# Graph attention with a sparse winner: index arithmetic on GpSimd, x loaded later, adj in halves and quarters, and another order of the drain

## The chip, the cores and the metric

The kernel runs on one core of one Trainium2 chip. The metric is the time of one execution on the device in microseconds (us). A profiled execution also gives a span, from the first to the last instruction of the core; the time on the device is a little longer than the span. Engines are named as in the profile: PE is TensorE (matmul), PEld its weight load, DVE VectorE, ACT ScalarE, POOL GpSimd, and SP SyncE, which here only issues transfers.

## The reference

One layer of graph attention with a residual and a layer norm:

```
ht  = (x @ W) per head                   # x 4096x512, W 512x(4*512)
e   = leaky_relu(src_i + dst_j) + adj    # adj 4096x4096
att = softmax(e, axis=-1)
y   = mean over heads of (att @ ht)
out = layernorm(x + y)
```

The entries of `adj` are either 0 or random numbers of up to 1e9. The largest entry of a row therefore outweighs all others by far more than the attention logits can reach, so the softmax of row i is 1 at the column of that entry and 0 elsewhere. Then `y[i]` is `x[col(i)] @ mean_h(W_h)`. The kernel computes this, and proves with a bound on the logits that every row has such a winner; if one had none, a general routine would follow, which is not entered with these inputs.

## The kernel before

Rows are taken in 32 blocks of 128; the row of partition p in block b is 32p + b. A block's `adj` is a tile of 128 x 4096 numbers of 4 bytes, 2 MB. All 32 blocks of x, and later of the output, live in one large tile, `hold`; W lies at first in the half of `hold` where x of blocks 16 to 31 will come. The order of all instructions on each engine is written out by hand, and each engine runs its own in order.

The main loop runs over steps t = 0 to 31. In a step:

- SP issues, when the table `x_at` says so, a load of x for four blocks (`load_x`, L109, 1 MB), and then the load of adj for block t+5 (`load_adj`, L106) into one of six buffers. Blocks 0 and 31 are loaded in four pieces, the others in one.
- DVE takes the maximum of each of 64 segments of 64 columns (`segment_maxima`, L149, two reductions a block), then finds the largest segment (`find_segment`, L156 and L158) and the number of its row in a table of segments (`row`, L160). POOL gathers that segment for all 128 rows (`lead`, L162).
- Between the two reductions DVE finds, for block t-2, the place inside the gathered segment (`find_column`, L176 and L181) and the column number (`col`, L183); POOL gathers the row of x with that number (`y`, L170).
- For block t-3, PE turns y (`project`, L206), ACT copies it out (`yt`, L213), PE adds x with an identity matrix (residual, L199) and multiplies with the mean of W (L219, eight instructions).
- For block t-4, ACT takes sum and sum of squares (`stats`, L231 and L233). For two blocks, t-6 and t-5, every second step, the normalisation factor is made (`rstd`: Sqrt on ACT L236, reciprocal and product on DVE L237 and L238), and ACT writes the normalised rows (`finish`, L242).
- `row_norm` (L226) squares and sums rows of x on ACT for the bound; `bound` (three parts), `test` and `count` make from it the proof that each row has a winner.

After the loop comes the drain: the columns of the last two blocks, of which block 31 is searched in its whole row of 4096 (`find_column_in_row`, L191), so that it needn't wait for its segment; the last blocks' projection and normalisation (`finish_last` with bn_stats, L248 to L257); and the stores of `hold` (L260): blocks 0 to 23 singly on SP, 24 to 27 in one of 1 MB, and the last four singly, the last of them on ACT's queue.

Of the kernel before, what the change touches and what calls it, by code (L numbers as in the profile page):

```python
# [9 lines left out]
F32 = mybir.dt.float32  # L10
U32 = mybir.dt.uint32
# [6 lines left out]
EPS = 1e-5  # L18
LOWEST = -3.4028234663852886e38
P = 128  # L20
# [45 lines left out]
def leading_rows(ctx, tc, x, adj, W, a, out, ident, v, n_bad, any_bad):  # L66
# [11 lines left out]
    AHEAD = 5  # L78
    Q = 4
    PIECES = 4  # L80

    once = ctx.enter_context(tc.tile_pool(name="once", bufs=1))
    adj_pool = ctx.enter_context(tc.tile_pool(name="adj_pool", bufs=AHEAD + 1))
# [14 lines left out]

    adj_t = {}

    def load_adj(ib):
        if 0 <= ib < NB:
            t = adj_t[ib] = adj_pool.tile([P, N], F32, name="adj_t")
            n = PIECES if ib in (0, NB - 1) else 1
            for k in range(n):
                nc.sync.dma_start(t[:, ts(k, N // n)], adj_rows[ib][:, ts(k, N // n)])  # L106

# [14 lines left out]
        load_adj(ib)  # L122

    make_identity(nc, ident)
    first_i = once.tile([P, NB], I32, name="first_i")
    nc.gpsimd.iota(first_i, pattern=[[S, NB]], base=0, channel_multiplier=NB * S)
    first = once.tile([P, NB], F32, name="first")
    nc.gpsimd.tensor_copy(first, first_i)
    ones = once.tile([P, P], F32, name="ones")
    nc.gpsimd.memset(ones, 1.0)  # L130
    eps = once.tile([P, 1], F32, name="eps")
    nc.gpsimd.memset(eps, EPS)

# [4 lines left out]
    sd = once.tile([P, NB], F32, name="sd")  # L138
    lead_by = once.tile([P, 1], F32, name="lead_by")

    seg_of, at_of, lead_of, y_t, o_ps = {}, {}, {}, {}, {}

    def segment_maxima(ib, lo, hi):

        if lo == 0:
            seg_of[ib] = small.tile([P, S], F32, name="seg")
        n = PIECES if ib in (0, NB - 1) else 2
        for k in range(lo * n // PIECES, hi * n // PIECES):
            nc.vector.tensor_reduce(  # L149
                seg_of[ib][:, ts(k, S // n)],  # L150
                adj_t[ib][:, ts(k, N // n)].rearrange("p (s e) -> p s e", e=E), axis=AX.X, op=OP.max,
            )

    def find_segment(ib):
        seg = seg_of.pop(ib)
        nc.vector.max(out=top[:, ib, :], in_=seg)  # L156
        at = small.tile([P, 8], U32, name="at")
        nc.vector.max_index(at, top[:, ib, :], seg)  # L158
        row = small.tile([P, 1], U32, name="row")
        nc.vector.tensor_tensor(row, at[:, 0:1], first[:, ib : ib + 1], op=OP.add)  # L160
        lead = small.tile([P, E], F32, name="lead")
        nc.gpsimd.indirect_dma_start(  # L162
            out=lead, out_offset=None, in_=adj_segs,
            in_offset=bass.IndirectOffsetOnAxis(ap=row[:, :1], axis=0),
        )
        at_of[ib], lead_of[ib] = at, lead

    def gather_rows(ib, col):
        y = y_t[ib] = rows.tile([P, D], F32, name="y", bufs=4)
# [5 lines left out]
    def find_inner(ib):  # L175
        nc.vector.max(out=inner[:, ib, :], in_=lead_of[ib])  # L176

    def find_column(ib):
        find_inner(ib)
        within = small.tile([P, 8], U32, name="within")  # L180
        nc.vector.max_index(within, inner[:, ib, :], lead_of.pop(ib))  # L181
        col = small.tile([P, 1], U32, name="col")
        nc.vector.scalar_tensor_tensor(  # L183
            col, at_of.pop(ib)[:, 0:1], float(E), within[:, 0:1], op0=OP.mult, op1=OP.add
        )
        gather_rows(ib, col)

    def find_column_in_row(ib):

        col = small.tile([P, 8], U32, name="col")  # L190
        nc.vector.max_index(col, top[:, ib, :], adj_t[ib])  # L191
        gather_rows(ib, col)

    def project(ib, between=(), order="turn residual"):

        o = o_ps[ib] = psum.tile([P, D], F32, name="o")

        def residual():
            nc.tensor.matmul(o, ident, hold[:, ib, :], start=True, stop=False)  # L199

        if order == "residual turn":
            residual()
        y = y_t.pop(ib)
        tp = psum.tile([P, KB, P], F32, name="tp", bufs=2)
        for kb in range(KB):
            nc.tensor.transpose(tp[:, kb, :], y[:, ts(kb, P)], ident)  # L206
        yt = rows.tile([P, KB, P], F32, name="yt")
        if order == "residual turn":
            half = KB // 2
            nc.scalar.copy(yt[:, :half, :], tp[:, :half, :])  # L210
            nc.vector.tensor_copy(yt[:, half:, :], tp[:, half:, :])
        else:
            nc.scalar.copy(yt, tp)  # L213
        if order == "turn residual":
            residual()
        for some in between:
            head_vector(*some)
        for kb in range(KB):
            nc.tensor.matmul(  # L219
                o, yt[:, kb, :], w_sum[:, kb, :],  # L220
                start=(kb == 0 and order == "turn"), stop=(kb == KB - 1),
            )

    def row_norm(ib):
        sq = rows.tile([P, D], F32, name="sq")
        nc.scalar.activation(sq, hold[:, ib, :], AF.Square, accum_out=xx[:, ib : ib + 1])  # L226
# [6 lines left out]
        nc.scalar.activation(sq, o, AF.Square, bias=nm[:, i], accum_out=sd[:, i])  # L233

    def rstd(i):
        nc.scalar.activation(sd[:, i], sd[:, i], AF.Sqrt, bias=eps, scale=1.0 / D)  # L236
        nc.vector.reciprocal(sd[:, i], sd[:, i])  # L237
        nc.vector.tensor_mul(nm[:, i], nm[:, i], sd[:, i])  # L238

    def finish(ib):  # L240
        i = slice(ib, ib + 1)
        nc.scalar.activation(hold[:, ib, :], o_ps.pop(ib), AF.Identity, bias=nm[:, i], scale=sd[:, i])  # L242
# [16 lines left out]
    def store(queue, lo, n):  # L259
        queue.dma_start(out_rows[:, ds(lo, n), :], hold[:, ds(lo, n), :])  # L260
# [25 lines left out]
    def head_vector(kb, h, wt):  # L286

        for k in range(KB):
            nc.tensor.matmul(  # L289
                pv[:, kb, h : 2 * H : H], wt[:, k, :], at_d[:, k, h : 2 * H : H],  # L290
                start=(k == 0), stop=(k == KB - 1),
            )
# [45 lines left out]
    def count():  # L338
        pg = psum.tile([1, NB], F32, name="px", bufs=1)
        nc.tensor.matmul(pg, ones[:, 0:1], gap, start=True, stop=True)  # L340
        nc.vector.tensor_scalar(n_bad, pg, -1.0, float(P), op0=OP.mult, op1=OP.add)
        total = once.tile([1, 1], F32, name="total")
        nc.vector.tensor_reduce(total, pg, axis=AX.X, op=OP.add)
        nc.vector.tensor_scalar(any_bad, total, -1.0, float(N), op0=OP.mult, op1=OP.add)

    x_at = {1: 1, 4: 2, 8: 3, 11: 4, 14: 5, 18: 6, 21: 7}
    norms_at = {t: [t - 2] for t in range(2, 18)}
    for k in range(8):
        norms_at[20 + k] = [16 + 2 * k, 17 + 2 * k]
    vectors = [(kb, h) for kb in range(KB) for h in range(H)]  # L350
    vectors_at = {t: 2 if t < 3 else 1 for t in range(1, 15)}
    COLUMN, PROJECT, STATS, FINISH = 2, 3, 4, 6
# [1 line left out]
    for t in range(NB):  # L354
        if t in x_at:
            load_x(x_at[t])
        load_adj(t + AHEAD)
        middle = 1 if t == NB - 1 else 2
        segment_maxima(t, 0, middle)
        if t >= COLUMN:  # L360
            find_column(t - COLUMN)
        segment_maxima(t, middle, PIECES)
        find_segment(t)
        pair = t >= FINISH and t % 2 == 0
        if pair:
            rstd(slice(t - FINISH, t - FINISH + 2))
        if t < 2:
            mean_of_heads(t)
        elif t == 2:
            mean_of_heads(2)  # L370
            mean_of_heads(3)
        if t == 0:
            turn_a()
        turned = [(*vectors[0], turn_w(*vectors.pop(0))) for _ in range(vectors_at.get(t, 0))]
        if t == 16:
            head_norms()
        if 28 <= t <= 30:
            bound(t - 28)
        if t >= PROJECT:
            project(t - PROJECT, turned)  # L380
        else:
            for some in turned:
                head_vector(*some)
        if pair:
            finish(t - FINISH)
            finish(t - FINISH + 1)
        if t >= STATS:
            stats(t - STATS)
        for ib in norms_at.get(t, ()):
            row_norm(ib)  # L390

    find_column(NB - 2)
    find_column_in_row(NB - 1)
    rstd(slice(NB - FINISH, NB - FINISH + 2))
    for ib in range(NB - 2 * Q):
        store(nc.sync, ib, 1)
    finish(NB - FINISH)
    finish(NB - FINISH + 1)
    store(nc.sync, NB - 2 * Q, Q)
    project(NB - 3, order="turn")  # L400
    find_inner(NB - 1)
    test()
    stats(NB - 4)
    rstd(slice(NB - 4, NB - 3))
    finish(NB - 4)
    store(nc.sync, NB - 4, 1)
    finish_last(NB - 3, True)
    store(nc.sync, NB - 3, 1)
    project(NB - 2, order="turn")
    count()  # L410
    finish_last(NB - 2, True)
    store(nc.sync, NB - 2, 1)
    project(NB - 1, order="residual turn")
    finish_last(NB - 1, False)
    store(nc.scalar, NB - 1, 1)

# [233 lines left out]
```

## Time and profile before

| What | Value |
|---|---|
| median of 14 runs | 259.67 us (258.35 to 261.43) |
| the profiled execution's time | 259.07 us |
| its span | 257.3 us |
| PE busy | 203.4 us (79%) |
| DVE busy | 200.2 us (78%) |
| ACT busy | 115.2 us (45%) |
| POOL busy | 62.0 us (24%) |
| bytes moved | 97.76 MB, 380 GB/s over the span |
| adj loads, issue to landing, median | 33.4 us (2 MB), 6.4 us (0.5 MB) |
| gathers, issue to landing, median | 6.7 us (`lead`), 8.3 us (`y`) |
| segment maxima, 128 x 2048 | 2280 ns each, 60 of them |
| granted PE clock, mean | 0.958 |

Busy times are averages over the whole span and don't say what bounds a stage; the views that do are slices and stretches of time, and the chain of waits, which is followed back from the last instruction. A share of the DMA engines near 1 means that all 16 were transferring. A transfer's time from issue to landing includes the time that it stood behind others in its queue.

### The profile page before, as it was taken

The page shows a single profiled execution, that of the slowest core. Times are in us where ns is not written, and L with a number is a line of the kernel's source. Part 1 is how long each engine was busy: PE and PEld are TensorE (multiplying, and loading weights), DVE is VectorE, ACT ScalarE, POOL GpSimd, SP SyncE. Part 2 cuts the span into 40 slices and gives each one's busy share as a digit, 9 for nine tenths or more (in the row PEclk, how much of TensorE's full clock was granted, in tenths as well). Part 3 has the DMA queues.
Part 4 walks back from the last instruction along what each step waited for, and adds up shares of the span by engine and source line. Part 5 has one row for each costly group of instructions (what it writes and reads, how often), then busy time and mean ns, then how long its engine had stood idle before and what let it go on. Part 6 is the DMA issues. An engine that isn't in the chain of part 4 may idle for free.

```text
span 257.3 us, 2464 instructions
## 1 busy us (share of the span) xinstructions
PE 203.4 (79%) x679; PEld 101.9 (40%) x680; DVE 200.2 (78%) x387; ACT 115.2 (45%) x285; POOL 62.0 (24%) x75
## 2 busy tenths in 40 slices
PE   0199869999899899989498788897785889939760
PEld 0136327665455556645143333332332334413320
DVE  2546777469979997996989999799799999972341
ACT  2012005356646475737264537584656555642110
POOL 1101221122322322232122233313313332320000
PEclk9999779999999999999979999999999999976996
DMA  6999999999999999999999999999999999997111
GB/s 250 415 433 420 412 425 422 410 428 420 416 416 422 418 415 414 427 410 416 423 411 425 415 421 418 414 423 414 415 420 416 418 393 399 383 376 290 41 41 52
DMA packets 14995, 97.76 MB, mean 380 GB/s; under 512 B 2296, under 2 KB 2296, under 8 KB 9472
## 3 DMA queue, kind: packets, MB, share of 16 engines
q1 hardware_dynamic: 11232, 87.82, 82.8%
q0 software_dynamic: 3584, 9.44, 9.6%
q10 hardware_dynamic: 160, 0.28, 0.3%
q8 instruction: 7, 0.11, 0.2%
q14 instruction: 12, 0.10, 0.1%
HBM read 89.15 MB, written 8.39 MB: 379 GB/s over the span
## 4 chain that ended last, share of the span: by engine, by line
DMA 57%; DVE 31%; PE 5%; issue 2%; ACT 1%; SPq 1%; POOLq 0%
DMA adj_t<-in_adj_dram 55%; DVE seg L149 21%; PE o L219 5%; DVE col L191 2%; DMA y<-in_x_dram,col 1%; DVE within L181 1%; DVE at L158 1%; DVE top L156 1%; DVE st L251 1%; DVE col L183 1%; DVE inner L176 1%; DVE row L160 1%; ACT hold L242 1%; SPq L106 1%; DVE hold L248 1%
## 5 line engine op out<-in xcount | busy, mean ns | idle before, releaser
L149 DVE TENSOR_REDUCE seg<-adj_t 128x32 f32<-128x2048 f32 (+1 forms) x68 | 146.3, 2155 | 30.3 <-DMA adj_t<-in_adj_dram 30.2
L219 PE MATMUL o<-w_sum,yt 128*128 128x512 f32 x256 | 121.4, 618 | 7.2 <-ACT yt L213 6.1
L219 PEld LDWEIGHTS o<-w_sum,yt 128*128 128x128 f32 x256 | 47.6, 196 | 67.3 <-issue 48.4
L170 POOL DMA_INDIRECT y<-in_x_dram,col x32 | 30.3, 947 | 99.1 <-issue 77.0
L162 POOL DMA_INDIRECT lead<-in_adj_dram,row x32 | 30.4, 951 | 68.5 <-DVE row L160 44.2
L213 ACT COPY yt<-tp 128x512 f32<-128x512 f32 x31 | 18.2, 586 | 42.4 <-PE tp L206 42.3
L206 PE MATMUL tp<-ident,y 128*128 128x128 f32 x128 | 19.8, 277 | 17.3 <-DMA y<-in_x_dram,col 17.3
L265 PE MATMUL o<-hold,ident 128*128 128x512 f32 x32 | 20.9, 813 | 15.6 <-DMA hold<-in_L_gnn_W_dram 15.6
L199 PE MATMUL o<-hold,ident 128*128 128x512 f32 x60 | 31.3, 604 | 0.0
L206 PEld LDWEIGHTS tp<-ident,y 128*128 128x128 f32 x128 | 14.3, 141 | 30.2 <-issue 27.9
L242 ACT ACTIVATE hold<-o,nm,sd 128x512 f32<-128x512 f32 x29 | 21.1, 781 | 6.0 <-DVE nm L238 6.0
L283 ACT COPY wt<-tp 128x512 f32<-128x512 f32 x16 | 9.2, 586 | 25.5 <-PE tp L281 25.5
L226 ACT ACTIVATE sq<-hold 128x512 f32<-128x512 f32 x32 | 19.8, 619 | 1.7 <-DMA hold<-in_x_dram 1.7
L233 ACT ACTIVATE sq<-o,nm 128x512 f32<-128x512 f32 x29 | 19.9, 687 | 0.9
L289 PEld LDWEIGHTS pv<-at_d,wt 128*128 128x128 f32 x128 | 16.3, 191 | 6.8 <-issue 3.8
L265 PEld LDWEIGHTS o<-hold,ident 128*128 128x128 f32 x32 | 8.1, 264 | 25.6 <-issue 20.6
L266 ACT ACTIVATE w_sum<-o 128x512 f32<-128x512 f32 x4 | 2.4, 599 | 34.2 <-PE o L265 34.2
L231 ACT ACTIVATE sq<-o 128x512 f32<-128x512 f32 x29 | 17.5, 605 | 0.0
L289 PE MATMUL pv<-at_d,wt 128*128 128x2 f32 x128 | 15.3, 244 | 0.6 <-ACT wt L283 0.6
L281 PEld LDWEIGHTS tp<-ident,hold 128*128 128x128 f32 x64 | 7.9, 142 | 6.9 <-issue 6.9
L281 PE MATMUL tp<-ident,hold 128*128 128x128 f32 x64 | 9.3, 273 | 0.0
L199 PEld LDWEIGHTS o<-hold,ident 128*128 128x128 f32 x60 | 9.1, 191 | 0.1
(73 smaller groups left out, 94.5 us busy)
## 6 DMA issues: line engine op xcount, KB each, us to landing
adj_t<-in_adj_dram SPq DMA_DIRECT2D x30, 2048.0 KB, 33.4
hold<-in_x_dram SPq DMA_DIRECT2D x8, 1024.0 KB, 33.8
out_dram<-hold SPq DMA_DIRECT2D x27, 256.0 KB, 5.5
adj_t<-in_adj_dram SPq DMA_DIRECT2D x8, 512.0 KB, 6.4
hold<-in_L_gnn_W_dram SPq DMA_DIRECT2D x4, 1024.0 KB, 17.8
out_dram<-hold SPq DMA_DIRECT2D x1, 1024.0 KB, 6.4
lead<-in_adj_dram,row POOLq DMA_INDIRECT x32, 6.7
y<-in_x_dram,col POOLq DMA_INDIRECT x32, 8.3
```

Source lines behind the costliest of these rows:

```text
L149: nc.vector.tensor_reduce(seg_of[ib][:, ts(k, S // n)], adj_t[ib][:, ts(k, N // n)].rearrange("p (s e) -> p s e", e=E), axis=AX.X, op=OP.max,)
L162: nc.gpsimd.indirect_dma_start(out=lead, out_offset=None, in_=adj_segs, in_offset=bass.IndirectOffsetOnAxis(ap=row[:, :1], axis=0),)
L170: nc.gpsimd.indirect_dma_start(out=y, out_offset=None, in_=x, in_offset=bass.IndirectOffsetOnAxis(ap=col[:, :1], axis=0),)
L199: nc.tensor.matmul(o, ident, hold[:, ib, :], start=True, stop=False)
L206: nc.tensor.transpose(tp[:, kb, :], y[:, ts(kb, P)], ident)
L213: nc.scalar.copy(yt, tp)
L219: nc.tensor.matmul(o, yt[:, kb, :], w_sum[:, kb, :], start=(kb == 0 and order == "turn"), stop=(kb == KB - 1),)
L226: nc.scalar.activation(sq, hold[:, ib, :], AF.Square, accum_out=xx[:, ib : ib + 1])
L233: nc.scalar.activation(sq, o, AF.Square, bias=nm[:, i], accum_out=sd[:, i])
L242: nc.scalar.activation(hold[:, ib, :], o_ps.pop(ib), AF.Identity, bias=nm[:, i], scale=sd[:, i])
L265: nc.tensor.matmul(o, ident, hold[:, w_at + kb * H + h, :], start=(h == 0), stop=(h == H - 1))
L289: nc.tensor.matmul(pv[:, kb, h : 2 * H : H], wt[:, k, :], at_d[:, k, h : 2 * H : H], start=(k == 0), stop=(k == KB - 1),)
```

## The change

- `row` and `col` are computed on POOL as integer additions. A further POOL multiplication, `start`, makes 64 times the segment number ahead of time. The table `first` is made directly as integers.
- `rstd` is computed on POOL: a scale and addition, a power of -0.5, and a product. ACT's Sqrt and DVE's reciprocal and product leave the loop; they stay in the drain's `finish_last`.
- adj is loaded and reduced in halves, block 0 and the last four blocks in quarters. (Before, all but two blocks were loaded whole and reduced in halves.)
- x of blocks 4g to 4g+3 is loaded at step 4g-2, for g = 1 to 6. x of the last four blocks is loaded after all of adj. `row_norm` of a block follows its `stats`; the last four follow in the drain, and `bound` with them.
- `project` is split into `turn`, `residual` and `products`. Blocks 28 to 30 get their x by an addition on DVE in `finish_last`, block 28 now too; block 31 gets it on PE between its turn and its products.
- The drain has a new order. Blocks 0 to 11 are stored singly on SP, behind the last x. Blocks 12 to 27 are stored in four transfers of 1 MB on ACT's queue, issued behind the copy of the turned y of block 31. The last four are stored as before.

```diff
+    LATE = NB - Q
+    def pieces(ib):
+        return PIECES if ib == 0 or ib >= LATE else PIECES // 2
...
-            n = PIECES if ib in (0, NB - 1) else 1
+            n = pieces(ib)
...
-        n = PIECES if ib in (0, NB - 1) else 2
+        n = pieces(ib)
...
-        nc.vector.tensor_tensor(row, at[:, 0:1], first[:, ib : ib + 1], op=OP.add)
+        nc.gpsimd.tensor_tensor(row, at[:, 0:1], first[:, ib : ib + 1], op=OP.add)
...
+        start = at_of[ib] = small.tile([P, 1], U32, name="start")
+        nc.gpsimd.tensor_tensor(start, at[:, 0:1], width, op=OP.mult)
...
-        nc.vector.scalar_tensor_tensor(
-            col, at_of.pop(ib)[:, 0:1], float(E), within[:, 0:1], op0=OP.mult, op1=OP.add
-        )
+        nc.gpsimd.tensor_tensor(col, at_of.pop(ib), within[:, 0:1], op=OP.add)
...
-        nc.scalar.activation(sd[:, i], sd[:, i], AF.Sqrt, bias=eps, scale=1.0 / D)
-        nc.vector.reciprocal(sd[:, i], sd[:, i])
-        nc.vector.tensor_mul(nm[:, i], nm[:, i], sd[:, i])
+        nc.gpsimd.tensor_scalar(sd[:, i], sd[:, i], 1.0 / D, EPS, op0=OP.mult, op1=OP.add)
+        nc.gpsimd.tensor_tensor(sd[:, i], sd[:, i], power[:, : i.stop - i.start], op=OP.pow)
+        nc.gpsimd.tensor_mul(nm[:, i], nm[:, i], sd[:, i])
...
-    x_at = {1: 1, 4: 2, 8: 3, 11: 4, 14: 5, 18: 6, 21: 7}
-    norms_at = {t: [t - 2] for t in range(2, 18)}
-    for k in range(8):
-        norms_at[20 + k] = [16 + 2 * k, 17 + 2 * k]
+    x_at = {4 * g - 2: g for g in range(1, NB // Q - 1)}
```

The drain after the change, whole (before it: see the end of the function above):

```
load_x(NB // Q - 1)
for ib in range(3 * Q):
    store(nc.sync, ib, 1)
find_column(NB - 2)
rstd(slice(NB - FINISH, NB - FINISH + 2))
find_column_in_row(NB - 1)
turn(NB - 3)
products(NB - 3, 0, KB - 1)
finish(NB - FINISH)
finish(NB - FINISH + 1)
for ib in range(LATE, NB):
    row_norm(ib)
turn(NB - 2)
products(NB - 3, KB - 1, KB)
bound(0)
products(NB - 2)
finish_last(NB - 4, True)
find_inner(NB - 1)
bound(1)
finish_last(NB - 3, True)
bound(2)
test()
turn(NB - 1)
for g in range(3, LATE // Q):
    store(nc.scalar, g * Q, Q)
residual(NB - 1)
products(NB - 1, 0, KB - 1)
pg = count()
products(NB - 1, KB - 1, KB)
for ib in (NB - 4, NB - 3):
    store(nc.sync, ib, 1)
finish_last(NB - 2, True)
store(nc.sync, NB - 2, 1)
report(pg)
finish_last(NB - 1, False)
store(nc.scalar, NB - 1, 1)
```

## The prediction

> **What bounds the kernel now.** I read the page's slices first, then busy times in stretches, the chain of waits, the groups of DVE and GpSimd (POOL), and the timeline of the last 40 us.
>
> ```profile
> DVE  2546777469979997996989999799799999972341
> DMA  6999999999999999999999999999999999997111
> ...
> 187.00:219.00 32.00, 26.38 (x77) 11.70 (x77) 30.97 (x64) 18.19 (x47) 9.46 (x10) 1.00 1.01 409
> 219.00:232.00 13.00, 9.03 (x27) 4.18 (x26) 10.93 (x24) 6.92 (x18) 3.79 (x4) 0.88 1.03 377
> 232.00:258.00 26.00, 14.46 (x36) 5.99 (x34) 7.39 (x20) 2.87 (x9) 0.00 (x0) 0.83 0.26 100
> ```
>
> In the slices the DMA engines are full from slice 1 to slice 36 (36 x 6.43 = 231 us and some more), then nearly empty. The stretches (length; PE, PEld, DVE, ACT, POOL busy; PE clock; DMA share; GB/s) say the same: 409 and 377 GB/s up to 232 us, 100 after. So there are two stages: one with bytes as its limit, and a drain of some 20 us in which one chain of small steps runs.
>
> ```profile
> 223.75 0.22 DVE within L181
> 224.00 0.16 DVE col L183
> 224.16 4.41 DVE col L191 x2
> 228.56 0.07 DVE sd L237
> 228.66 0.17 DVE nm L238
> 228.83 0.03 issue
> 228.86 1.45 ACT hold L242 x2
> 230.31 0.48 ACT yt L213
> 230.79 0.04 issue
> 230.83 6.16 PE o L219 x8
> ...
> 239.50 3.70 PE o L219 x8
> ...
> 246.03 3.71 PE o L219 x8
> ...
> 251.24 0.81 DVE hold L257
> ```
>
> That is the drain: the column search of the last block (4.41), then the normalisation factor of blocks 26 and 27 queued behind that search on DVE, ACT's finish of them, and only then three blocks' products one after another, up to the last store at 252.1 us.
>
> When does adj end? Ahead of its last byte go 67.1 MB of adj, 4.2 of W, 8.4 of x and some 28 pairs of gathers (9.44 MB/32 = 0.295 MB a pair): 88.0 MB. The rates of the stretches 0:9, 9:40, 40:77, 77:122, 122:153, 153:187 (285, 424, 419, 418, 418, 416 GB/s) and 187:219 times their lengths give 90.2 MB by 219 us. The 2.2 MB too many are stores; 2.2/0.41 = 5 us back gives about 214 us. DVE ends the last segment maxima at 222.7 us: it sits one block behind, because a 2 MB tile counts only when it is whole (about 5.7 us of transfer, and 5.95 us of DVE work from 186.8 to 222.7 over six blocks).
>
> **What the Trainium skill says.** "GPSIMD Engine Reference", section "Performance versus the Vector engine": Pool pays two software hops per instruction and about 2.6 cycles an element of a two-input operation. At one or two elements a lane only the fixed part counts; the trace agrees in size (POOL CAST of 128x32: 211 ns, memset of one column: 93). "SBUF — State Buffer", section "SBUF: two separate sides": DVE and GpSimd share a port pair that one of them locks for a whole instruction, in DVE's case when it is in a two-port mode or has two SBUF inputs. The segment maxima read 2048 elements in 2280 ns, about 0.9 a ns, which is one port's rate, and POOL's gather starts stay at 943 to 950 ns beside them: I see no lock in this trace. "DMA: Bandwidth & Descriptors", section "Issuing engines are not separate DMA queues": transfers of SP, ACT and GpSimd run on the same 16 engines and interleave. The trace agrees: share 1.01 with GpSimd's queue at 9.6%. So no byte becomes cheaper by changing queue. "TensorE: Matmul & The Clock Gate", section "What's actually happening": after an idle window of about 3.4 us PE falls to half clock. Here PE idled some 4 us before 230.83, and the eight products took 6.16 us instead of 3.70.
>
> **The change, part by part.**
>
> *Row, column and factor to GpSimd.*
>
> ```profile
> L160 DVE TENSOR_TENSOR row<-at,first 128x1 uint32<-128x1 uint32 x32 | 5.1, 159 | 1.2
> L183 DVE SCALAR_TENSOR_TENSOR col<-at,within 128x1 uint32<-128x1 uint32 x31 | 4.9, 160 | 1.1
> L238 DVE TENSOR_TENSOR nm<-nm,sd 128x2 f32<-128x2 f32 x14 | 2.2, 161 | 0.5
> L237 DVE RECIPROCAL sd<-sd 128x2 f32<-128x2 f32 x14 | 2.2, 157 | 0.0
> ```
>
> DVE loses 5.1 + 4.9 + 2.2 + 2.2 = 14.4 us, 0.45 a block: 5.95 becomes about 5.5. Bytes set the pace at about 6.2 us a block where x is loaded and 5.7 where not, so this saves nothing directly; it keeps DVE from sliding. ACT loses its small Sqrt (0.29 x 14), which is not on the path. POOL gains three small operations a block (row, start, column) and three a pair for the factor, say 0.2 us each. Per pair POOL then has 4 gather starts x 0.95, 2.1 us of start delays (0.26 after row, 0.76 after col), 6 x 0.2 and 3 x 0.2: 7.7 us of 11.4 to 12.4. The factor waits on POOL for ACT's statistics, and the next gathers stand behind it; those statistics are a step old by then, so I count no wait. The power, on two elements a lane, has no row in this trace: not below 0.1 us (the smallest memset), and free up to about 4 us, where POOL would be full. I take 0.3. The step from index to gather start stays about equal: one hop DVE to POOL in either case, +0.1.
>
> *x later, the last four blocks' x behind adj.* Seven x loads instead of eight stand ahead of adj's end: 1.05 MB/0.41 = 2.6 us earlier. x of block 4g lands just ahead of adj of block 4g+2; PE wants it three steps after block 4g, so it is not late.
>
> *Halves and quarters.* SP issues about twice as many loads (0.33 us each, on a queue that mostly waits). Rows become 8 KB, late ones 4 KB. 9:40, where W and x in 8 KB rows are half of the bytes, ran at 424 GB/s; 219:232, mostly stores in 2 KB rows, at 377. So 8 KB costs between 0 and 3.3 us on 54 MB; I take 1.3. The late 4 KB rows cost 0 to 1.5; I take 0.7. Adj then ends at A = 214 - 2.6 + 2.0 = 213.4 us. The gain is what follows: DVE no longer begins a block when it is whole. After the last quarter come one 1.21 us reduction and 0.6 of search, were there nothing else.
>
> *The drain, counted from A.* Within the last block DVE stops for lead of block 29 (segment found about A-8.3, plus 0.3 start and 6.7 landing), until A-1.3; three quarters later, at A+2.8, the maxima are done and at A+3.4 the segment. Lead of block 30 was asked for at A-2.9 and lands at A+4.1; its column takes until A+4.7; then the 4.41 us search, A+9.2. The factor no longer queues behind it. The gather of y for block 31 starts at A+9.4 and lands in 5.6 to 8.3 us, I take 7: A+16.4, against a start at 229.3 before, now 222.8.
>
> PE: y of block 28 lands at about A+2.8, its work ends at A+8; block 29 from A+8 to A+12 with three of four products; y of block 30 lands at A+13; the four moved row norms (4 x 0.8 on ACT, behind the two finishes and a copy) end near A+14, so the moved bound's transpose goes then (0.27 on PE, its two reductions 0.5 on DVE, beside the products), and the products of block 30 (3.7) end near A+18.7. Blocks 28 and 29 are now added and normalised on DVE, 2.6 us each (0.69 + 0.69 + 0.18 + 0.29 + 0.16 + 0.55), beside PE. Block 31 is turned behind block 30's products, not when its y lands: turned and copied (0.6 + 0.6) at A+20.3. Then residual 1.0, products 3.7, count 0.2, and DVE's 0.70 + 0.19 + 0.30 + 0.17 + 0.81 with hops: the last store is ready at A+27.
>
> But ACT issues the stores of blocks 12 to 27 only behind that copy, at A+20.3, and the last store stands on ACT's queue behind them. Queue SP ends x (1.05 MB) and twelve stores (3.1 MB) with the gathers at about A+13.6: some 7 us of empty DMA. From A+20.3: 0.4 issue, about 1 to the first byte, then 4.2 MB and the last blocks' 1.05 less 0.5 that SP has stored by then, 4.7 MB at 0.40 = 11.8 us: A+33.5. What follows a last byte: before, the store's issue ended at 252.5 and the span at 257.3; less 1 to the first byte and 0.65 of transfer, 3.2 us. So the span is 213.4 + 36.7 = 250.1 us, 7.2 less than 257.3. The profiled execution took 259.07, 1.8 more than its span, and the median is 259.67, 0.6 above that: 252.5 us.
>
> **Rivals.**
>
> *The compute chain ends last* (15 in 100). If the stores of ACT finish by A+31 because some of them start sooner (y of 31 early, PE less behind), the last store decides: A+27 + 0.4 + 4.8 = A+32.2, span 245.6, 248.0 us. For it: only 4 us separate the two ends. Against: the order puts all four big stores behind the last turn.
>
> *Packets and cold PE eat half* (12 in 100). 8 and 4 KB rows at their upper bound add 2.8 us to A, and half clock on one block in the drain (6.16 - 3.70 = 2.5) passes to the stores: 252.5 + 5 = 257.5. For it: 377 GB/s with short rows, and the clock fell in this very stage before. Against: 424 GB/s with half the bytes in 8 KB rows.
>
> *GpSimd becomes the pace: slower* (11 in 100). One mechanism: the power, run per block pair in POOL's order ahead of the next gathers. Beyond the 4 us that fit, each further us costs about 13 us over 13 pairs: the 7.2 us gained are gone at about 4.6 us, and at 6 us the time is 252.5 + 26 = 278 us. For it: no such operation is in the trace and the skill calls GpSimd's loops software. Against: two elements, and all of POOL's fixed costs seen are under 0.3 us.
>
> *The gather or the drain does not move* (6 in 100): lead or y land so late that the search order counts for nothing, 259 to 260 us. Against: 4.41 us and the factor behind it are plain in the chain.
>
> **How the numbers follow.** Forecast 56 in 100, own range 249 to 256 (A by -1.5 to +2.5, start of the stores by -2 to +2). With the first two rivals 248.0 to 257.5 hold over 80 in 100. About 0.3% (0.8 us) is what can be told from no change. Faster: 56 + 15 + 12 and 1 of the last rival, 84; same 4; slower 12.
>
> **What would show it.** Right: the last segment maxima end near 216 instead of 222.7; in the slices the DMA digits fall for one slice near 228 to 233 and fill again; ACT's queue holds four 1 MB stores issued near 234; POOL's power under 1 us. Wrong: segment maxima that wait for something other than adj in mid-kernel; GB/s clearly under 410 between 40 and 190 us; POOL near full; DMA full without a gap, in which case the time is under 249.

## The result and the profile after

| | before | after |
|---|---|---|
| median | 259.45 us (47 runs) | 254.97 us (253.86 to 256.15, 10 runs) |
| ratio to before | | 0.983, 95% interval 0.980 to 0.985 |
| profiled execution, time and span | 259.07, 257.3 us | 255.6, 253.7 us |

The change makes the kernel 1.7% faster. The forecast was 252.5 us (2.7%), in a range of 248.0 to 257.5: right in direction and in its main mechanism, and too good by 2.5 us.

The slices of the changed kernel (40 of 6.34 us; digits are tenths of busy time, the last row GB/s):

```profile
DVE  2586657695999489958898989589958999845820
POOL 1203233244455345544444544525652464640000
...
DMA  7999999999999999999999999999999999980793
GB/s 251 431 417 416 413 416 412 410 415 418 408 410 408 417 411 410 414 408 414 413 415 408 413 410 411 408 417 412 413 407 403 404 401 409 403 309 29 305 413 114
```

Before, the DMA engines were full up to about 236 us and then nearly idle to the end. Now they are full up to about 226, nearly empty in one slice (29 GB/s), and full again nearly to the end. The gap that the prediction described, the empty stretch ahead of the last stores, is there, and what it said would follow it, too.

The same in stretches, for the changed kernel (length; PE, PEld, DVE, ACT, POOL busy; PE clock, DMA share, GB/s):

```profile
77.00:122.00 45.00, 45.00 (x187) 26.08 (x186) 36.43 (x56) 29.34 (x71) 20.18 (x44) 1.00 1.02 412
...
187.00:216.00 29.00, 23.34 (x67) 10.14 (x68) 24.47 (x44) 13.49 (x33) 14.29 (x31) 1.00 1.02 405
216.00:226.00 10.00, 7.77 (x19) 3.35 (x18) 7.87 (x11) 5.87 (x15) 5.46 (x13) 0.83 1.04 393
226.00:236.00 10.00, 9.33 (x32) 4.47 (x31) 4.27 (x12) 5.68 (x16) 0.93 (x1) 1.00 0.24 84
236.00:251.00 15.00, 4.64 (x12) 1.44 (x10) 5.98 (x22) 1.13 (x3) 0.00 (x0) 0.78 0.84 336
```

And for the kernel before, in two of these stretches:

```profile
77.00:122.00 45.00, 42.90 (x180) 24.79 (x179) 40.54 (x76) 27.32 (x68) 13.25 (x14) 1.00 1.01 418
...
226.00:236.00 10.00, 6.03 (x12) 2.73 (x12) 4.46 (x12) 4.37 (x9) 0.95 (x1) 0.66 1.00 380
```

Two things are to be read here. In mid-kernel the full DMA engines move 412 GB/s instead of 418, though their share is as high: the shorter rows cost something all the way. And between 226 and 236 us the load is now the other way round: PE busy 9.33 of 10 us, DMA 0.24.

The order of the drain, from the timeline of ACT of the changed kernel (ACTq is ACT's instruction queue; such a line issues a transfer):

```profile
235.95 0.59 ACT L206 COPY yt<-tp 128x512 f32<-128x512 f32 x1
235.96 3.12 ACTq L258 DMA_DIRECT2D out_dram<-hold  x4
239.42 0.29 ACT L253 ACTIVATE r<-mv,eps 128x1 f32<-128x1 f32 x1 [2.88 <-DVE mv L251]
241.71 0.29 ACT L253 ACTIVATE r<-mv,eps 128x1 f32<-128x1 f32 x1 [2.00 <-DVE mv L251]
243.08 0.34 ACTq L258 DMA_DIRECT2D out_dram<-hold  x1
```

The four 1 MB stores are issued with the copy of block 31, at 236 us. The last block's store is ready at 243.1, 9 us earlier than before (252.1), but it stands behind 4.2 MB on its own queue, and the span ends 10.6 us later. Before, 5.2 us passed from that issue to the end:

```profile
252.08 0.39 ACTq L260 DMA_DIRECT2D out_dram<-hold  x1
```

### The profile page after: what moved, and what is told of

It is laid out like the page before. It is cut to its first block, busy times and chain, and to the rows that moved or that the text cites. A ratio compares the mean times of both kernels' runs of the same rounds, so it can differ in the third digit from the quotient of the medians.

```text
span 253.7 us, 2541 instructions
## 1 busy us (share of the span) xinstructions
PE 203.4 (80%) x677; PEld 102.3 (40%) x678; DVE 189.2 (75%) x304; ACT 109.6 (43%) x266; POOL 97.9 (39%) x213
## 4 chain that ended last, share of the span: by engine, by line
DMA 43%; POOL 16%; issue 16%; DVE 9%; PE 6%; ACT 5%; POOLq 0%; DVEq 0%
DMA adj_t<-in_adj_dram 38%; DMA hold<-in_L_gnn_W_dram 6%; PE o L217 5%; POOL lead L168 5%; POOL y L178 5%; DVE seg L155 4%; POOL sd L235 2%; ACT hold L240 2%; ACT sq L224 1%; DVE st L249 1%; POOL start L173 1%; POOL row L166 1%; DVE hold L255 1%; POOL col L191 1%; DVE hold L246 1%
## 5 line engine op out<-in xcount | busy, mean ns | idle before, releaser
L217 PE MATMUL o<-w_sum,yt 128*128 128x512 f32 x256 | 123.2, 624 | 7.4 <-ACT yt L206 7.4
L178 POOL DMA_INDIRECT y<-in_x_dram,col x32 | 32.3, 1008 | 17.1 <-POOL col L191 15.2
L263 PE MATMUL o<-hold,ident 128*128 128x512 f32 x32 | 18.7, 737 | 16.0 <-DMA hold<-in_L_gnn_W_dram 16.0
L210 PE MATMUL o<-hold,ident 128*128 128x512 f32 x58 | 30.9, 615 | 0.5 <-DMA hold<-in_x_dram 0.5
L240 ACT ACTIVATE hold<-o,nm,sd 128x512 f32<-128x512 f32 x28 | 20.3, 779 | 19.9 <-POOL nm L236 19.9
L166 POOL TENSOR_TENSOR row<-at,first 128x1 uint32<-128x1 uint32 x32 | 5.9, 186 | 53.0 <-DVE at L164 51.9
L191 POOL TENSOR_TENSOR col<-start,within 128x1 uint32<-128x1 uint32 x31 | 5.9, 190 | 38.2 <-DVE within L189 37.3
L287 PEld LDWEIGHTS pv<-at_d,wt 128*128 128x128 f32 x128 | 17.2, 200 | 7.3 <-ACT wt L281 3.7
L263 PEld LDWEIGHTS o<-hold,ident 128*128 128x128 f32 x32 | 7.3, 241 | 24.7 <-POOL row L166 10.6
L229 ACT ACTIVATE sq<-o 128x512 f32<-128x512 f32 x28 | 16.9, 605 | 0.0
L287 PE MATMUL pv<-at_d,wt 128*128 128x2 f32 x128 | 16.0, 249 | 0.6 <-ACT wt L281 0.6
```

Source lines behind the costliest of these rows:

```text
L178: nc.gpsimd.indirect_dma_start(out=y, out_offset=None, in_=x, in_offset=bass.IndirectOffsetOnAxis(ap=col[:, :1], axis=0),)
L210: nc.tensor.matmul(o_ps[ib], ident, hold[:, ib, :], start=True, stop=False)
L217: nc.tensor.matmul(o_ps[ib], yt_of[ib][:, kb, :], w_sum[:, kb, :], start=(start and kb == 0), stop=(kb == KB - 1),)
L263: nc.tensor.matmul(o, ident, hold[:, w_at + kb * H + h, :], start=(h == 0), stop=(h == H - 1))
L287: nc.tensor.matmul(pv[:, kb, h : 2 * H : H], wt[:, k, :], at_d[:, k, h : 2 * H : H], start=(k == 0), stop=(k == KB - 1),)
```

## The experiments

All ratios are to the kernel before, timed beside it on the same chip, with 95% intervals. The chips differ from group to group, so kernels are compared by their ratios. Each expectation names a theory, A, and a rival.

| kernel | median us | ratio |
|---|---|---|
| after | 254.97 | 0.983 (0.980 to 0.985) |
| e1_whole: adj mostly whole | 254.42 | 0.982 (0.978 to 0.986) |
| e4_no_pool | 254.87 | 0.984 (0.980 to 0.988) |
| e7_x_early | 256.76 | 0.990 (0.986 to 0.993) |
| e9_drain_only | 255.28 | 0.983 (0.979 to 0.988) |
| e5_before_halves | 259.19 | 0.997 (0.994 to 1.000) |
| e2_stores_sp | 264.94 | 1.022 (1.018 to 1.026) |
| e6_fill: stores on SP | 249.73 | 0.961 (0.957 to 0.966) |
| e8_fill_whole | 249.08 | 0.959 (0.954 to 0.964) |
| e10_drain_filled | 254.70 | 0.979 (0.972 to 0.985) |
| e12_fill_whole_no_pool | 251.76 | 0.969 (0.964 to 0.974) |
| e11_earlier | 250.20 | 0.965 (0.960 to 0.971) |
| e13_one_factor | 251.66 | 0.974 (0.970 to 0.978) |

### Which part brings the gain

**e1_whole**, adj of blocks 1 to 27 loaded whole:

```diff
-            n = pieces(ib)
+            n = PIECES if ib == 0 or ib >= LATE else 1
             for k in range(n):
                 nc.sync.dma_start(t[:, ts(k, N // n)], adj_rows[ib][:, ts(k, N // n)])
```

> The changed kernel, but adj of blocks 1 to 27 is loaded whole again (reductions stay in halves, the last four blocks stay in quarters). Theory A (the shorter rows cost the DMA rate): 417 to 419 GB/s between 9 and 187 us instead of 411 to 416, adj's last byte some 2.5 to 3 us earlier, near 213; the drain moves less, as DVE is again most of a block behind when the late blocks come, so 252 to 255.5 us. Rival (the rate fell for another reason, such as GpSimd's instructions): the rate stays at 411 to 412 and the time rises to 256 or more, because DVE starts each block later.

The rate came back, as this stretch shows:

```profile
77.00:122.00 45.00, 43.11 (x174) 24.47 (x173) 37.35 (x57) 28.43 (x69) 21.25 (x45) 1.00 1.01 418
```

In the records of single packets adj's last one ends at 215.62 us before, at 215.59 after and at 212.98 here. So x behind adj is worth its 2.6 us, and halves alone took 2.6 us back. The time hardly moved (254.42, intervals overlap). DVE ended its maxima only 0.9 us earlier than in the changed kernel, and ACT copied block 28's turned y 0.9 us earlier. The four stores were issued 2.5 us earlier (233.45), but 1.6 of that is PE's clock: block 28's products took 3.70 us in this profile and 5.30, partly at half clock, in that of the changed kernel. A profile holds one execution, and the mean granted clock varies between executions (0.928 to 0.969 in the six of this kernel). The 0.9 us are too little for the times to tell.

**e5_before_halves**, the pieces put into the kernel before:

```diff
+    def pieces(ib):
+        return PIECES if ib == 0 or ib >= NB - Q else PIECES // 2
...
-            n = PIECES if ib in (0, NB - 1) else 1
+            n = pieces(ib)
```

(and the same in the reductions)

> The kernel before, with adj in halves and the last four blocks in quarters, nothing else. Theory A (rows cost 3 us of adj's end, but DVE no longer lags by a block): rate 411 to 412, adj ends near 218, the last maxima end near 221 instead of 222.7, time 257 to 260. Rival (the pieces carry the gain of the whole change): 256 or less.

259.19 us, a ratio of 0.997: at most 0.6% faster, of the 1.7% of the whole change. Pieces alone carry little of the gain. What the expectation says of the rate and of the maxima is left open.

**e4_no_pool**, row, column and factor back where they were:

```diff
-        nc.gpsimd.tensor_tensor(row, at[:, 0:1], first[:, ib : ib + 1], op=OP.add)
+        nc.vector.tensor_tensor(row, at[:, 0:1], first[:, ib : ib + 1], op=OP.add)
...
-        nc.gpsimd.tensor_scalar(sd[:, i], sd[:, i], 1.0 / D, EPS, op0=OP.mult, op1=OP.add)
-        nc.gpsimd.tensor_tensor(sd[:, i], sd[:, i], power[:, : i.stop - i.start], op=OP.pow)
-        nc.gpsimd.tensor_mul(nm[:, i], nm[:, i], sd[:, i])
+        nc.scalar.activation(sd[:, i], sd[:, i], AF.Sqrt, bias=eps, scale=1.0 / D)
+        nc.vector.reciprocal(sd[:, i], sd[:, i])
+        nc.vector.tensor_mul(nm[:, i], nm[:, i], sd[:, i])
```

> The changed kernel with row, column and factor back on DVE and ACT. Theory A (they only keep DVE from sliding): DVE goes from 5.45 to about 5.9 us a block, above the pace of blocks without x, so the last segment maxima end 1 to 3 us later than 218.3 and the time is 255.5 to 258. Rival (the hop through GpSimd costs as much as DVE saves: from the search to the gather's start it took about 0.8 us against 0.3 before): no difference or up to 1.5 us faster, 253.5 to 255.

254.87, as the changed kernel. Yet the search of block 31 starts 2.8 us later:

```profile
221.89 0.16 DVE L187 SCALAR_TENSOR_TENSOR col<-at,within 128x1 uint32<-128x1 uint32 x1
223.17 0.17 DVE L233 RECIPROCAL sd<-sd 128x2 f32<-128x2 f32 x1 [1.12 <-ACT sq L222]
223.37 0.16 DVE L234 TENSOR_TENSOR nm<-nm,sd 128x2 f32<-128x2 f32 x1
223.44 0.09 DVE L195 MATCH_VALUE_LOAD col<-top,adj_t 128x8 f32 x1
223.52 4.42 DVE L195 FIND_INDEX8 col<-top,adj_t 128x8 uint32<-128x4096 f32 x1
```

The factor stands ahead of the search on DVE and waits 1.1 us for ACT. So theory A's delay was there and its price was not: in this drain the search is not on the way to the end. Block 28's products, from which the end follows (see e9_drain_only), began only 0.3 us later than in the changed kernel (220.99 instead of 220.65).

**e7_x_early**, `x_at` of the kernel before, all eight loads ahead of adj's end:

```diff
-    x_at = {4 * g - 2: g for g in range(1, NB // Q - 1)}
+    x_at = {1: 1, 4: 2, 8: 3, 11: 4, 14: 5, 18: 6, 21: 7}
...
-    load_x(NB // Q - 1)
```

> The changed kernel with the loads of x at the steps of the kernel before, all eight ahead of adj's end. Theory A (bytes decide when the drain begins): adj ends 2.6 us later, near 218, and so does everything behind it: 256.5 to 258. Rival (DVE and PE are behind by more than that, so adj's last byte is not what the drain waits for): within 1 us of 255.0.

Adj's last packet 2.6 us later (218.2), as expected; the time 256.76, 0.7 points above the changed kernel's ratio, about 1.8 us of the 2.6: within theory A's range.

**e9_drain_only** undoes all three: no GpSimd arithmetic, x at the old steps, adj in the old pieces.

> The changed kernel with row, column and factor on DVE and ACT, x loaded at the old steps and adj in the old pieces: of the change only the new drain is left. Theory A (the drain is the gain, and the other parts matter little because the stores of ACT end last): 255 to 257. Rival (the parts each bring some 1 to 2 us): 257.5 to 259.5, near the kernel before.

255.28, ratio 0.983, the ratio of the whole change. The new drain alone (with the row norms in their new places, which this run keeps) brings the whole gain, and the other parts together nothing that shows. In it the search starts at 224.6 us, 3.9 us after that of the changed kernel, and the gather of y for block 31 at 229.8, and still ACT issues the four stores at the same time, from its timeline:

```profile
235.77 3.11 ACTq L256 DMA_DIRECT2D out_dram<-hold  x4
```

Block 31 is turned behind the products of block 30. The last packet of its gather ends at 232.8 us, and the turn starts at 235.1: the search and this gather have slack. PE's work from block 28 on has none. In the profiles of the changed kernel, e1, e4, e7 and e9 the stores are issued 10.0 to 10.2 us behind the end of block 28's products, and the span ends 17.5 to 18.0 us behind that. So with the stores where they are, the end moves with block 28's products.

What the new order takes out is a wait of PE. Before, it waited 3.97 us for the copy of block 29's y, which stood on ACT behind the finish of blocks 26 and 27, and so behind the 4.42 us search; here it waits 0.67. The first line is of the kernel before, the second of e9_drain_only:

```profile
230.83 6.14 PE L219 MATMUL o<-w_sum,yt 128*128 128x512 f32 x8 [3.97 <-ACT yt L213]
226.87 2.84 PE L215 MATMUL o<-w_sum,yt 128*128 128x512 f32 x6 [0.67 <-ACT yt L204]
```

What each move of the drain is worth by itself was not tried.

### The stores that the end waits for

**e2_stores_sp** moved the four large stores to SP behind the twelve single ones, a line too early.

```diff
     for ib in range(3 * Q):
         store(nc.sync, ib, 1)
+    for g in range(3, LATE // Q):
+        store(nc.sync, g * Q, Q)
...
-    for g in range(3, LATE // Q):
-        store(nc.scalar, g * Q, Q)
```

> The changed kernel, but the four 1 MB stores of blocks 12 to 27 go on SP right behind the twelve single ones instead of on ACT behind the copy of block 31. Theory A (the empty DMA from 227 to 237 us is what the end waits for): the gap fills, the last bytes are those of block 31, the last store stays ready near 243 us, span 247.5 to 249.5, time 249 to 251. Rival (the gap is needed, since the last two gathers of y are slowed by stores): y of blocks 30 and 31 lands 2 us or more later, PE waits for it, and the time is 253 or more.

264.94 us, slower than both. The kernel stores blocks 26 and 27 before they are normalised, so it leaves out the normalisation of these two in the output; and their finish, later in the program, must wait until the store has read them. Its timeline of ACT:

```profile
226.30 0.59 ACT L206 COPY yt<-tp 128x512 f32<-128x512 f32 x1 [3.91 <-PE o L217]
239.77 1.45 ACT L240 ACTIVATE hold<-o,nm,sd 128x512 f32<-128x512 f32 x2 [12.88 <-DMA out_dram<-hold]
241.11 0.62 ACT L224 ACTIVATE sq<-hold 128x512 f32<-128x512 f32 x1
```

ACT waits 12.88 us for a store, and the drain behind it. It neither supports nor refutes the gap; it shows what a store costs whose rows are still to be written.

**e6_fill** puts it right: blocks 12 to 23 behind the single stores, 24 to 27 behind the finish of block 27.

```diff
+    for g in range(3, LATE // Q - 1):
+        store(nc.sync, g * Q, Q)
...
     finish(NB - FINISH + 1)
+    store(nc.sync, LATE - Q, Q)
...
-    for g in range(3, LATE // Q):
-        store(nc.scalar, g * Q, Q)
```

> The changed kernel, with the 1 MB stores of blocks 12 to 23 on SP right behind the twelve single ones, and that of 24 to 27 on SP behind the finish of block 27; ACT issues only the last store. Theory A (the end waits for stores that were issued at 236 us into empty DMA engines): no empty stretch from 227 to 237 us, the last store still ready near 243 us and the last to land, span 247.5 to 249.5, time 249 to 251. Rival (the gap protects the last two gathers): they land 2 us or more later, PE waits for them, time 253 or more.

249.73 us, 3.9% faster than before and 2.1 points below the change. Its stretches:

```profile
216.00:226.00 10.00, 6.61 (x20) 2.65 (x18) 7.73 (x10) 6.34 (x17) 5.17 (x12) 1.00 1.04 400
226.00:236.00 10.00, 8.86 (x28) 4.26 (x29) 5.12 (x16) 5.15 (x15) 1.07 (x1) 1.00 1.02 418
236.00:251.00 15.00, 4.76 (x13) 1.51 (x11) 5.33 (x18) 1.17 (x3) 0.00 (x0) 0.77 0.30 116
```

No gap, and the last store is issued at 243.12, as in the changed kernel (243.08). 5.2 us later the span ends, not 10.6. The rival is half right. The last gather of y lands 5.3 us later than in the changed kernel (its last packet ends at 234.7 instead of 229.4), and PE waits for y of blocks 29 and 31, as it did not there:

```profile
224.85 0.63 PE L204 MATMUL tp<-ident,y 128*128 128x128 f32 x4 [0.65 <-DMA y<-in_x_dram,col]
235.41 0.63 PE L204 MATMUL tp<-ident,y 128*128 128x128 f32 x4 [0.99 <-DMA y<-in_x_dram,col]
```

That the last store is ready at the same moment all the same is due to PE's clock: block 28's products took 3.70 us in this profile, not 5.30.

**e8_fill_whole**: both e6 and e1.

> Both edits: stores filled in on SP as in e6_fill, and adj of blocks 1 to 27 loaded whole as in e1_whole. Theory A: adj ends near 213, DVE's last maxima near 217.4, the chain of PE begins about 1 us earlier, and with no stores to wait for this shows: 0.5 to 1.5 us under e6_fill, 248 to 250.5. Rival (PE's chain from block 28 on is set by something else): equal to e6_fill within 0.4 us.

249.08, the fastest median of the study. The gain of 0.65 us over e6_fill lies in theory A's range, but the intervals overlap, so it isn't shown by the times. (In this profile block 28's products took 5.40 us, again partly at half clock.)

### What the other parts are worth once the stores are out of the way

**e10_drain_filled** is e9_drain_only with the stores of e6_fill.

> e9_drain_only (row, column and factor on DVE and ACT, x at the old steps, adj in the old pieces) with the stores filled in on SP as in e6_fill. Theory A (the other parts of the change were hidden by the late stores and show once these are gone): the gather of y for block 31 starts near 229.8 us as in e9, lands some 7 us later because stores now run beside it, and the chain behind it takes 8.3 us to the last store: 245.5, time 251.5 to 253. Rival (the parts bring nothing at all): 249 to 250.3, as e6_fill and e8_fill_whole.

Ratio 0.979, against 0.959 for e8_fill_whole: with the late stores gone the other parts of the change are worth about 2 points, some 5 us. The other way round, filling in the stores without these parts gains nothing that shows (0.979 against 0.983 for e9_drain_only, intervals overlap). The time, 254.70, lies above theory A's 251.5 to 253, and in the profile that is PE's clock, as e10's timeline of PE shows:

```profile
228.44 0.67 PE L202 MATMUL tp<-ident,y 128*128 128x128 f32 x4 [2.18 <-DMA y<-in_x_dram,col]
229.78 5.49 PE L215 MATMUL o<-w_sum,yt 128*128 128x512 f32 x6 [0.68 <-ACT yt L204]
```

Six products take 5.49 us instead of 2.84 (e6_fill), after a wait of 2.18 for a late gather, a turn and a copy.

**e12_fill_whole_no_pool** is e8_fill_whole without GpSimd's arithmetic.

> e8_fill_whole with row, column and factor back on DVE and ACT. Theory A (without the late stores the work on DVE counts): the search of block 31 starts 2 to 3 us later, as it did in e4_no_pool (223.5 us against 220.7), the gather behind it too, and the time is 250 to 251.5. Rival (PE's chain covers it): 248.5 to 249.5, as e8_fill_whole.

Ratio 0.969 against 0.959, with intervals that just touch: GpSimd's part seems to be worth about a point now, where it was worth nothing under the late stores (e4). e11_earlier below, which has this part and was timed on the same chip as e12, stands at 0.965, so the point is not firm. The last maxima end at 221.6 us instead of 217.4, so DVE has slid, and the factor makes it wait once more:

```profile
222.88 0.16 DVE L187 SCALAR_TENSOR_TENSOR col<-at,within 128x1 uint32<-128x1 uint32 x1
225.81 0.17 DVE L233 RECIPROCAL sd<-sd 128x2 f32<-128x2 f32 x1 [2.76 <-ACT sd L232]
226.01 0.16 DVE L234 TENSOR_TENSOR nm<-nm,sd 128x2 f32<-128x2 f32 x1
226.08 0.08 DVE L195 MATCH_VALUE_LOAD col<-top,adj_t 128x8 f32 x1
226.16 4.42 DVE L195 FIND_INDEX8 col<-top,adj_t 128x8 uint32<-128x4096 f32 x1
```

**e13_one_factor** is e12 with this one factor on GpSimd.

> e12_fill_whole_no_pool, with the factor of blocks 26 and 27 in the drain alone on GpSimd; all other rows, columns and factors stay on DVE and ACT. Theory A (what GpSimd brings is mostly this one factor: on DVE it stood ahead of the 4.42 us search and waited 2.76 us for ACT in e12): the search of block 31 starts near 223.2 us instead of 226.2, and the ratio to the kernel before falls from 0.969 to 0.960 to 0.966. Rival (it is DVE's time in every step): the search starts at 225 us or later, ratio 0.968 to 0.972.

The search does start 4.4 us earlier (221.7), 1.3 of it because the maxima ahead of it ended earlier in this profile (220.3 instead of 221.6). But the ratio is 0.974, no lower than e12's. Theory A fell: that wait was long in one profile, and removing it doesn't show in the times. The rival's late search did not come either. The maxima still end 2.8 us later than in e8_fill_whole (217.4), which leaves DVE's time in every step as the likelier source of GpSimd's point; the runs don't settle it.

**e11_earlier** is e8 with the factor ahead of `find_segment`, block 28's column a quarter earlier, and the four row norms ahead of the turn of block 29.

> e8_fill_whole with three moves: the factor of two blocks in front of find_segment on POOL instead of behind it, the column of block 28 after the first quarter of block 30, and the four last row norms ahead of the turn of block 29 on ACT. Theory A (PE's chain from block 28 on starts with the landing of y for blocks 28 and 29): both gathers start about 1 us earlier, and the end comes 0.7 to 1.5 us earlier: 247.3 to 248.5. Rival (the last gather, behind the 4.4 us search, sets the end): within 0.4 us of e8_fill_whole.

0.965 against 0.959, intervals overlapping: no gain. The first two turns did come earlier (block 28 at 216.95 us instead of 218.51), and PE then waited for the next gathers, in its timeline:

```profile
223.18 2.84 PE L217 MATMUL o<-w_sum,yt 128*128 128x512 f32 x6 [0.80 <-ACT yt L206]
228.59 0.63 PE L204 MATMUL tp<-ident,y 128*128 128x128 f32 x4 [2.56 <-DMA y<-in_x_dram,col]
...
234.20 0.63 PE L204 MATMUL tp<-ident,y 128*128 128x128 f32 x4 [0.27 <-DMA y<-in_x_dram,col]
```

That there is no gain is as the rival said; its reason is seen only in part. In this profile PE waits for the landing of y for blocks 30 and 31, and most for block 30 (2.56 us), whose gather does not stand behind the long search. e8_fill_whole waited for neither in its profile.

## Why the prediction was right, and where it was short

- *The end is the four stores on ACT, issued at the copy of block 31, with a gap in front.* Right, and the reason why the gain is no larger: e6_fill removes it and gains 5 us more. e6_fill changes both the time and the queue of these stores, and a late issue on SP was not run; but from 237 to 248 us the changed kernel moves about 410 GB/s, the rate of full engines, so the late start is cause enough.
- *The start of these stores* was put 20.3 us behind adj's end; measured 235.96 - 215.59 = 20.4. That this fits so well is in part luck. Block 28's work ended 10.4 us behind adj's end, not 8, and from there 10.0 us passed to the issue, not 12.3, because PE did not wait for y of block 30 and the row norms as the sum had it. Two things made block 28 late. Its products took 5.30 us instead of 3.70, although PE had waited only 0.74 and 1.49 us just before, not some 4 us as in the case that the prediction cites; so 1.6 of the 2.5 us of the rival "cold PE" (half clock) happened. And the factor: the prediction let GpSimd wait for ACT's statistics and counted nothing, but the wait was the other way round. ACT's finish of blocks 24 and 25 waited 2.63 us for the factor, and the copy of block 28's y stood behind it:

```profile
216.68 1.45 ACT L240 ACTIVATE hold<-o,nm,sd 128x512 f32<-128x512 f32 x2 [2.63 <-POOL nm L236]
...
220.65 5.30 PE L217 MATMUL o<-w_sum,yt 128*128 128x512 f32 x8 [1.49 <-ACT yt L206]
```

- *The rest of the drain, counted from adj's end.* Last maxima +2.8, measured +2.7 (218.3, where "near 216" was named as a sign: adj's end was later than put). Search +4.8, measured +5.1; last store ready +27, measured +27.5. The gather of block 31 started later than the sum (+10.3 for +9.4) and landed, counted to its last packet, in 3.5 us, not 7, into engines that were almost empty by then; it had slack either way.
- *Where it was short: adj's end.* It was put at A = 213.4 from 214 before; both kernels' last packet ends at 215.6. Of these 2.2 us, 1.6 are the starting point. It was counted from bytes as if no store came before adj's last packet, but 0.76 MB of stores, 1.8 us at 0.41 MB a us, had moved by then. The rest is the term "8 KB costs between 0 and 3.3 us; I take 1.3", which measured 2.6 (e1_whole), so that the pieces gave back all that the later x had gained. It leant on the stretch 9:40 with 424 GB/s, where 8 KB rows were said to be half of the bytes; by the packet records they were a third (4.2 of 13.1 MB), and with nearly all rows at 8 KB the changed kernel moves 416 there. The late 4 KB rows, taken as 0.7, seem to cost nothing: e1_whole has them, and its adj ends 2.6 us ahead of the kernel before, all of which the later x explains (e7_x_early). They were not tried alone.
- *Where it was short: the tail of the stores.* From the stores' issue to the end of the span 17.7 us passed instead of 16.4. SP had stored one of the last blocks by the time of the issue, not two, so 5.0 MB were left instead of 4.7, and the last packets came in thinly: 13.9 us passed from the first to the last, where 11.8 were put. Adj's end, this start and this tail, 2.2 + 0.1 + 1.3 = 3.6 us, are the whole difference in the span (253.7 against 250.1). The profiled execution lay 0.6 us above its median, where that of before lay below, hence 2.5 us in the medians.
- *Two readings of the kernel before* were off without harm. The DMA engines were full to about 236 us, not 232, and the first of the 64 gather starts took 1.12 us, not 0.95.
- *Row, column and factor "save nothing directly".* Right for this kernel (e4_no_pool), and the reason was too narrow: what they save is time ahead of the search of block 31, which has slack here, while the factor on GpSimd makes ACT wait as shown above. What the power costs, taken as 0.3 us with a bound of 4, is 0.72:

```profile
L235 POOL TENSOR_TENSOR sd<-sd,power 128x2 f32<-128x2 f32 x14 | 10.1, 724 | 1.2
L173 POOL TENSOR_TENSOR start<-at,width 128x1 uint32<-128x1 uint32 x32 | 6.5, 203 | 0.6
L166 POOL TENSOR_TENSOR row<-at,first 128x1 uint32<-128x1 uint32 x32 | 5.9, 186 | 53.0 <-DVE at L164 51.9 <-DVE v L293 1.2
L191 POOL TENSOR_TENSOR col<-start,within 128x1 uint32<-128x1 uint32 x31 | 5.9, 190 | 38.2 <-DVE within L189 37.3 <-PE tp L279 0.8
```

These groups of POOL (busy us and mean ns of one behind the bar) put the slower rival away: POOL is busy 39% of the span, and the small operations are 0.19 to 0.20 us, as assumed. The step from a search to its gather did stay about equal, as put (+0.1): in the medians it grew from 0.46 to 0.78 us for `lead` and fell from 0.96 to 0.81 for `y`.
- *The compute chain ends last* (15 in 100, 248.0 us): not in this kernel, but it is what e6_fill and e8_fill_whole become, at 249.7 and 249.1.

## What to carry to other kernels

When a drain has both stores and a chain of small steps, issue every store whose rows are final as soon as the queue's last load is issued. Here four stores queued behind an unrelated late step cost about 5 us at the end. But stores that fill the gap slow the last gathers: without the other parts of the change, filling gained nothing that shows. So judge the parts of a change again when what ends last has changed: here they were worth nothing that shows with the late stores and about 5 us without. A tile loaded in pieces starts its consumer earlier but pays for shorter rows over the whole kernel, here 2.6 us of adj's end, so it may belong only at the end, where the lag is seen; the times don't show that. And before comparing two profiles, look at the clock: half clock on one block is worth as much here as several of these parts.

## What the runs showed of the hardware

Rows of 8 KB instead of 16 KB lowered the rate of full DMA engines from 418 to 412 GB/s, and e1_whole's 16 KB rows brought 418 back; a packet of 8 KB took 320 ns on average, one of 16 KB 624. With the shorter rows in the same queues, the gathers landed sooner after their issue, in the median: `lead` 5.6 us instead of 6.7, `y` 7.0 instead of 8.3 (and 8.6 in e8_fill_whole, with long rows again). Counted to the last packet it is the same picture: 4.7 to 4.8 and 6.1 to 6.2 us in the kernels whose adj has 8 KB rows (after, e4, e6, e7), 5.5 to 5.9 and 7.1 to 7.3 in those with 16 KB (before, e1, e8, e9, e10, e12). The last gather of y, counted the same way, landed in 3.5 us into almost empty engines and in 8.5 beside stores (e6_fill). A power of two numbers in each of 128 partitions takes 724 ns on GpSimd, nearly four times an integer addition there. PE fell to half clock after waits of no more than 1.49 us, with only a turn between them: its clock record shows 0.5 from 220.5 to 223.9 us in the changed kernel.
